# Transposing gathered rows of an expert tile: sixteen block transfers and VectorE in place of four TensorE transposes

## The chip, the core and the metric

The kernel runs on one core of a Trainium2 chip. A core has a matrix engine (TensorE; PE in the profile, PEld its weight loads), a vector engine (VectorE, DVE), a scalar engine (ScalarE, ACT), GpSimd (POOL) and a sync engine (SP) that only waits and issues transfers. Each engine runs its own instructions in order; they meet through semaphores. Sixteen DMA engines move data between the chip's memory and SBUF, the core's on-chip memory of 128 partitions. The metric is the device time of one execution in microseconds (us), lower is better.

## The reference

One layer over 2048 tokens of width 512, in float32: a state-space (Mamba-2) block with a gated MLP, then a mixture of eight experts of which each token uses two. The part that matters here is the second.

```python
def _L0_ffn_ref(x, Wr, Wg, Wu, Wd):          # x: 1 x 2048 x 512, 8 experts, inner width 352
    router_logits = jnp.einsum('bsh,he->bse', x, Wr)
    probs = jax.nn.softmax(router_logits.astype(jnp.float32), axis=-1)
    topk_w, topk_idx = jax.lax.top_k(probs, K)
    topk_w = topk_w / jnp.sum(topk_w, axis=-1, keepdims=True)
    ...
    g = jnp.einsum('bsh,ehi->besi', x, Wg)
    u = jnp.einsum('bsh,ehi->besi', x, Wu)
    h = jax.nn.silu(g) * u
    y = jnp.einsum('besi,eih->besh', h, Wd)
    out = jnp.einsum('bse,besh->bsh', combine.astype(x.dtype), y)
    ...
x = x + _L0_attn_ref(_layernorm(x, axis=-1), ...)      # state-space block and gated MLP
x = x + _L0_ffn_ref(_layernorm(x, axis=-1), L0_ffn_Wr, L0_ffn_Wg, L0_ffn_Wu, L0_ffn_Wd)
```

## The kernel before, in words

The kernel works in three overlapping stages. `mamba` goes over eight blocks of 256 tokens. `feed_forward` goes over four blocks of 512 tokens, each in sixteen chunks of the inner width 2048; its weights pass through three buffers of the tag `mg` (tiles `mg` and `ms`, loaded by SP) and four of `md`. Each `feed_forward` ends with `route`, which normalises the rows (`xn`, line 598), writes them to `xnd` in memory (and to `xnd1` for the first three blocks), computes the router logits with `wr_sb`, and appends each token to the lists of its two experts by indirect scatters on POOL (line 669).

The expert stage computes only what is routed. The lists are cut into tiles of 128 rows of one expert. `table` turns the counts into a table of tiles: `first` has ten tiles (`NS1`) from the first three blocks of tokens, so that they can start while the last block is still routed; `rest` covers what is left, after a load of the lists on SP (line 973). 36 tiles (`NSA`) always run; three more stand under a condition at the end.

A tile s takes these steps:

- `gather` (line 1024, POOL): an indirect transfer fetches 128 rows of 512 values into `xg`, two buffers (tag `row3`).
- `front`: TensorE transposes the four 128 x 128 blocks of `xg` (`transposed`, line 201) into one PSUM bank `pt`, and ScalarE copies them to `xgT` (line 203). `xgT` has the 128 positions of the width on partitions, as the matmuls need.
- `hidden` (lines 1043, 1047, 1048): matmuls `epg` and `epu`, four of each, with the expert's weights `ew` chosen by a register; then Silu on ScalarE and a product on VectorE give `eh`.
- `turned` (lines 1055 to 1058): three transposes of `eh` on TensorE, copied to `ehT` by VectorE and ScalarE.
- `back` (lines 1064, 1069, 1070): three matmuls `epd`, VectorE scales by the token's weight to `ey`, and POOL scatters the rows with an addition into `out`.

`tiles` overlaps them: in iteration s it gathers ahead, does `front` for tile s + 1, the first half of `hidden` for s, `turned` for s - 1, the second half of `hidden`, and `back` for s - 1. `fetch` gathers one tile further than `front`. The last block's routing (`second`) is advanced along with it.

```python
            steps = hidden(s, xT.pop(s))
            next(steps)
            if last:
                hT = turned(s - 1, last[0])
            ...
            now = finish(steps)
            yield
            if last:
                if s < NSA - 1:
                    back(s - 1, hT, last[1])
```

TensorE's instructions stand in the order in which the program is written from block 2 on (`tc.manual_schedule`). The queues of the other engines, SP and POOL included, are ordered by a planner that works with assumed costs, so an instruction that waits holds up what the planner put behind it. The planner also sets the semaphores: transfers issued by SP and ACT take eight completion semaphores in turn, and one that takes a semaphore first waits for the transfer that had it.

Of the kernel before, what the change touches and what calls it, by code (L numbers as in the profile page):

```python
# [9 lines left out]
F32 = mybir.dt.float32  # L10
I32 = mybir.dt.int32
AF = mybir.ActivationFunctionType
ALU = mybir.AluOpType
# [3 lines left out]
P = 128  # L17
T = 2048
D = 512
NK = D // P  # L20
# [12 lines left out]
FC = 128  # L33
NFC = DFF // FC
NE = 8
EI = 352
ET = [(0, 128), (128, 128), (256, 96)]


NS = (2 * T + NE * (P - 1)) // P  # L40

NS1 = 10


NSA = (2 * T + NE * (P // 2)) // P
EW = NK * 2 * EI + len(ET) * D
EPS = 1e-5
# [7 lines left out]
def mamba_mlp_moe(ctx, tc, x, w_in, w_out, w_gu, w_down, par, wr, wg, wu, wd, out):  # L55
# [3 lines left out]
    nc = tc.nc  # L59

    def bc(ap, axis, n):
        ap = ap.unsqueeze(axis)
        shape = list(ap.shape)
        shape[axis] = n
        return ap.to_broadcast(shape)
# [7 lines left out]
    pmlp = ctx.enter_context(tc.tile_pool(name="pmlp", bufs=2, side="right"))  # L73
# [13 lines left out]
    w_o = pw.tile([P, 8, D], F32, name="w_o")  # L87
    wr_sb = const.tile([P, NK, NE], F32, name="wr_sb")

# [6 lines left out]
    def load_w_in(pair):  # L96
# [15 lines left out]
        out=tri, in_=ones, pattern=[[1, P]], compare_op=ALU.is_ge, fill=0.0, base=0, channel_multiplier=-1  # L112
# [3 lines left out]
        out=late, in_=ones, pattern=[[-1, P]], compare_op=ALU.is_gt, fill=0.0, base=0, channel_multiplier=1  # L116
# [3 lines left out]
    nc.gpsimd.memset(eps, EPS)  # L120
    rank = const.tile([P, NE], F32, name="rank")
    nc.gpsimd.iota(rank, pattern=[[-1, NE]], base=NE, channel_multiplier=0, allow_small_or_imprecise_dtypes=True)
    halo = pw.tile([P, 12, 3], F32, name="halo")
    nc.vector.memset(halo, 0.0)
    count = const.tile([P, P], F32, name="count")
    nc.gpsimd.iota(count, pattern=[[1, P]], base=0, channel_multiplier=0, allow_small_or_imprecise_dtypes=True)
    count_hi = const.tile([P, P // NE], F32, name="count_hi")
    nc.vector.tensor_scalar_mul(count_hi, count[:, 0 : P // NE], float(P))
# [4 lines left out]
        out=upto, in_=ones[:, : NE * NE].rearrange("p (e f) -> p e f", e=NE), pattern=[[1, NE], [-1, NE]],  # L133
# [8 lines left out]
    def rsqrt_eps(dst, src, scale=1.0):  # L142

        nc.scalar.activation(dst, src, AF.Sqrt, bias=eps, scale=scale)
        nc.vector.reciprocal(dst, dst)

    def stats(pool, src, dst):
        st = pool.tile([P, 6], F32, name="bn", tag="bn")
        nc.vector.bn_stats(out=st, in_=src)
        nc.vector.bn_aggr(out=dst, in_=st)  # L150
# [26 lines left out]
    def bank(kind, shape, name):  # L177
        pool, tag = use[kind]
        return pool.tile([P, *shape], F32, name=name, tag=tag)
# [17 lines left out]
    def transposed(src, dst, weight=None, kind="tr"):  # L197

        pt = bank(kind, [NK, P], "pt")
        for k in range(NK):  # L200
            nc.tensor.transpose(pt[:, k, :], src[:, k * P : (k + 1) * P], ident)  # L201
        if weight is None:
            nc.scalar.copy(dst, pt)  # L203
        else:
            nc.vector.tensor_tensor(dst, pt, bc(weight, 2, P), ALU.mult)
# [314 lines left out]
    KH = NK // 2  # L520
# [62 lines left out]
    def small(name, *shape):  # L583
        return small_p.tile([P, *shape], F32, name=name, tag=name)

    def route(fb, rows):

        mv2, rs2 = small("mv2", NJ, 2), small("rs2", NJ)
        for j in range(NJ):
            stats(small_p, rows[j], mv2[:, j, :])  # L590
        rsqrt_eps(rs2, mv2[:, :, 1])
        lg, l2, tmp = (small(n, NJ, NE) for n in ("lg", "l2", "tmp"))

        def normed(j):
            t = fb * NJ + j
            nc.scalar.dma_start(out=out[t * P : (t + 1) * P, :], in_=rows[j])
            xn = mid([D], f"xn{t}")
            nc.vector.tensor_scalar(xn, rows[j], mv2[:, j, 0:1], rs2[:, j : j + 1], ALU.subtract, ALU.mult)
            nc.scalar.dma_start(out=xnd[t * P : (t + 1) * P, :], in_=xn)
            if fb < NFB - 1:  # L600
                nc.scalar.dma_start(out=xnd1[t * P : (t + 1) * P, :], in_=xn)
            return xn

        def logits(j, xT):
            pl = bank("d", [NE], f"pl{fb}_{j}")
            for k in range(NK):
                nc.tensor.matmul(pl, xT[:, k, :], wr_sb[:, k, :], start=(k == 0), stop=(k == NK - 1))
            nc.vector.tensor_copy(lg[:, j, :], pl)

        xn = normed(0)  # L610
        yield
        for j in range(NJ):
            if j:
                logits(j - 1, xT)
            xT = mid([NK, P], f"xT{fb}_{j}")
            transposed(xn, xT)
            if j < NJ - 1:
                xn = normed(j + 1)
            yield
        logits(NJ - 1, xT)  # L620

        chosen = [small(n, NJ, NE) for n in ("o1", "o2")]
        m1, m2, *mr = (small(n, NJ) for n in ("rm1", "rm2", "mr1", "mr2"))

        def top(src, mx, mr, oh):

            nc.vector.tensor_reduce(mx, src, AX.X, ALU.max)
            nc.vector.tensor_tensor(tmp, src, bc(mx, 2, NE), ALU.is_equal)
            nc.vector.tensor_tensor(tmp, tmp, bc(rank, 1, NJ), ALU.mult)
            nc.vector.tensor_reduce(mr, tmp, AX.X, ALU.max)  # L630
            nc.vector.tensor_tensor(oh, tmp, bc(mr, 2, NE), ALU.is_equal)

        top(lg, m1, mr[0], chosen[0])
        nc.vector.scalar_tensor_tensor(l2, chosen[0], -3.0e38, lg, ALU.mult, ALU.add)
        top(l2, m2, mr[1], chosen[1])

        wt = [small(n, NJ) for n in ("wt1", "wt2")]
        nc.vector.tensor_tensor(m2, m2, m1, ALU.subtract)
        nc.scalar.activation(m2, m2, AF.Exp)
        nc.vector.tensor_scalar_add(wt[0], m2, 1.0)  # L640
        nc.vector.reciprocal(wt[0], wt[0])
        nc.vector.tensor_tensor(wt[1], m2, wt[0], ALU.mult)


        both, prior = small("both", NJ, NE), small("prior", NJ, NE)
        nc.vector.tensor_tensor(both, *chosen, ALU.add)
        nc.vector.tensor_copy(prior[:, 0, :], before)
        for j in range(1, NJ):
            nc.vector.tensor_tensor(prior[:, j, :], prior[:, j - 1, :], both[:, j - 1, :], ALU.add)
        nc.vector.tensor_tensor(before, prior[:, NJ - 1, :], both[:, NJ - 1, :], ALU.add)  # L650
        yield
        yield
        pr = bank("tr", [NJ, NE], f"pr{fb}")
        nc.tensor.matmul(pr, tri, both, start=True, stop=False)
        nc.tensor.matmul(pr, ones, prior, start=False, stop=True)
        nc.vector.tensor_copy(prior, pr)

        for n in range(2):

            at, to = small("at", NJ), small_p.tile([P, NJ], I32, name=f"to{n}", tag=f"to{n}")  # L660
            nc.vector.tensor_tensor(tmp, chosen[n], prior, ALU.mult)
            nc.vector.tensor_reduce(at, tmp, AX.X, ALU.add)
            nc.vector.scalar_tensor_tensor(at, mr[n], -float(T), at, ALU.mult, ALU.add)
            nc.vector.tensor_scalar_add(at, at, NE * T - 1.0)
            nc.vector.tensor_copy(to, at)
            entry = entries[:, n, fb * NJ : (fb + 1) * NJ, :]
            nc.vector.tensor_copy(entry[:, :, 1], wt[n])
            for j in range(NJ):
                nc.gpsimd.indirect_dma_start(
                    out=writers.pop(), out_offset=bass.IndirectOffsetOnAxis(ap=to[:, j : j + 1], axis=0),  # L670
                    in_=entry[:, j, :], in_offset=None,
                )
            yield
# [240 lines left out]
    ew = pexp.tile([P, NE, EW], F32, name="ew")  # L914
    NG = NK * 2 * EI

    def load_expert(e, part):

        gu = ew[:, e, :NG].rearrange("p (k a n) -> p k a n", k=NK, a=2)
        d = ew[:, e, NG:].rearrange("p (m n) -> p m n", m=len(ET))  # L920
        for lo in (part * EI,) if part < 2 else (NG, NG + 2 * D):
            nc.gpsimd.tensor_copy(ew[: EI - 2 * P, e, lo : lo + 1], newest[: EI - 2 * P, 0:1])
        if part < 2:
            nc.sync.dma_start(out=gu[:, :, part, :], in_=(wg, wu)[part][e].rearrange("(k p) n -> p k n", p=P))
        else:
            nc.sync.dma_start(out=d[:, 0:2, :], in_=wd[e, 0 : 2 * P, :].rearrange("(k p) n -> p k n", p=P))
            nc.sync.dma_start(out=d[: EI - 2 * P, 2, :], in_=wd[e, 2 * P : EI, :])

# [98 lines left out]
        return xg  # L1027

    def front(s, xg):
        xT = wk.tile([P, NK, P], F32, name=f"xgT{s}", tag="a", bufs=4)  # L1030
        transposed(xg, xT)
        return xT

    def hidden(s, xT):
        n, (exp_i, _, _, _), _ = of(s)
        e = nc.tensor.value_load(exp_i[0:1, n : n + 1], min_val=0, max_val=NE - 1)
        w = ew[:, bass.DynSlice(e, 1), :].rearrange("p a n -> p (a n)")
        pg = bank("g", [EI], f"epg{s}")
        pu = bank("u", [EI], f"epu{s}")
# [37 lines left out]
    got, xT = {}, {}  # L1077
# [114 lines left out]
```

## Time and profile before

| what | value |
|---|---|
| time, median of 3 runs | 1545.49 us (1543.01 to 1547.49) |
| the profiled execution | 1548.72 us, span of its instructions 1546.9 us |
| mean granted TensorE clock | 0.991 of full speed |
| busy share of the span | PE 97%, DVE 48%, ACT 48%, POOL 27% |
| expert stage | from about 1231 us to the end |

The profile is of one execution. It lists each instruction's engine, line, operation and its tiles as `out<-in`; `SPq` is SP issuing a transfer, and a transfer's landing is told apart from its issue. A busy TensorE is a row of overlapping matmuls, so the length of one instruction is longer than what it adds. Waits are put down to whoever ended them last.

### The profile page before, as it was taken

The page shows a single profiled execution, that of the slowest core. Times are in us where ns is not written, and L with a number is a line of the kernel's source. Part 1 is how long each engine was busy: PE and PEld are TensorE (multiplying, and loading weights), DVE is VectorE, ACT ScalarE, POOL GpSimd, SP SyncE. Part 2 cuts the span into 40 slices and gives each one's busy share as a digit, 9 for nine tenths or more (in the row PEclk, how much of TensorE's full clock was granted, in tenths as well). Part 3 has the DMA queues.
Part 4 walks back from the last instruction along what each step waited for, and adds up shares of the span by engine and source line. Part 5 has one row for each costly group of instructions (what it writes and reads, how often), then busy time and mean ns, then how long its engine had stood idle before and what let it go on. Part 6 is the DMA issues. An engine that isn't in the chain of part 4 may idle for free. (4 is left out here: it accounts for less than half of the span.)

```text
span 1546.9 us, 18821 instructions
## 1 busy us (share of the span) xinstructions
PE 1501.2 (97%) x6153; PEld 1022.8 (66%) x6153; DVE 747.7 (48%) x1937; ACT 744.1 (48%) x1332; POOL 423.9 (27%) x537
## 2 busy tenths in 40 slices
PE   7999999999999999999999999999999999999996
PEld 6656667677767676766776777666776665566553
DVE  7676866554645564547454553434343432222221
ACT  5888967635764597548646653222221221111110
POOL 3532324424332212141212121311121133333321
PEclk9999999999999999999999999999999999999998
DMA  9444445545554554354335632436878434333332
GB/s 295 146 135 124 136 147 188 188 156 158 169 164 145 173 179 140 104 128 157 123 126 161 186 100 89 93 106 218 292 184 269 150 75 58 69 68 63 63 66 35
DMA packets 128241, 217.54 MB, mean 141 GB/s; under 512 B 12560, under 2 KB 72848, under 8 KB 128144
## 3 DMA queue, kind: packets, MB, share of 16 engines
q1 hardware_dynamic: 105376, 166.34, 35.6%
q0 software_dynamic: 9088, 18.91, 7.2%
q10 hardware_dynamic: 13680, 31.07, 5.4%
q8 instruction: 52, 0.85, 0.2%
q14 instruction: 45, 0.37, 0.1%
HBM read 175.48 MB, written 40.80 MB: 140 GB/s over the span
## 5 line engine op out<-in xcount | busy, mean ns | idle before, releaser
L691 PE MATMUL pd<-md,a 128*128 128x512 f32 x512 | 238.9, 593 | 0.8 <-DVE r L692 0.7
L340 PE MATMUL pm<-hT,wi 128*128 128x256 f32 x768 | 185.7, 387 | 5.2 <-DMA wi<-in_w_in 5.2
L340 PEld LDWEIGHTS pm<-hT,wi 128*128 128x128 f32 x768 | 142.0, 192 | 30.8 <-issue 8.0
L692 DVE TENSOR_TENSOR r<-r,pd 128x512 f32<-128x512 f32 x128 | 87.5, 684 | 151.9 <-PE pd L691 148.4
L691 PEld LDWEIGHTS pd<-md,a 128*128 128x128 f32 x512 | 97.1, 190 | 76.8 <-issue 65.8
L361 DVE SCALAR_TENSOR_TENSOR ca<-pre,params,ca 128x256 f32<-128x256 f32 x288 | 142.4, 553 | 0.3
L707 PE MATMUL py<-h2T,ms 128*128 128x256 f32 x512 | 132.5, 381 | 3.4 <-DMA ms<-late 2.7
L772 POOL TENSOR_TENSOR a<-a,up 128x256 f32<-128x256 f32 x64 | 46.9, 734 | 267.6 <-DVE up L766 234.7
L340 PE MATMUL pz<-hT,wi 128*128 128x256 f32 x512 | 117.0, 381 | 0.0
L490 PE MATMUL po<-w_o,zs 128*128 128x512 f32 x256 | 112.7, 593 | 0.0
L1043 PE MATMUL epg<-ew,xgT 128*128 x288 | 109.0, 460 | 0.2 <-ACT xgT L203 0.2
L707 PEld LDWEIGHTS py<-h2T,ms 128*128 128x128 f32 x512 | 96.1, 191 | 19.2 <-issue 3.1
L1043 PE MATMUL epu<-ew,xgT 128*128 x288 | 108.7, 459 | 0.0
L420 ACT ACT_TABLE_LOAD x75 | 96.2, 1283 | 21.7 <-DVE ncum L285 14.1
L340 PEld LDWEIGHTS pz<-hT,wi 128*128 128x128 f32 x512 | 94.8, 190 | 13.8 <-ACT cum L420 0.8
L1064 PE MATMUL epd<-ew,ehT 128*128 (+1 forms) x216 | 100.6, 602 | 1.0 <-DVE ehT L1057 1.0
L420 ACT ACTIVATE cum<-cum,ncum 128x128 f32<-128x128 f32 x256 | 85.7, 392 | 7.3 <-POOL cum L314 6.0
L490 PEld LDWEIGHTS po<-w_o,zs 128*128 128x128 f32 x256 | 48.4, 190 | 56.1 <-issue 55.0
L752 ACT COPY a<-px 128x256 f32<-128x256 f32 x64 | 23.6, 369 | 126.4 <-PE px L707 113.1
L1024 POOL DMA_INDIRECT xg<-xnd,idx x36 | 35.9, 996 | 163.4 <-PE pt L201 161.2
L203 ACT COPY xgT<-pt 128x512 f32<-128x512 f32 x36 | 21.0, 587 | 116.5 <-PE pt L201 116.5
L422 DVE SCALAR_TENSOR_TENSOR cum<-cum,dt,psc 128x128 f32<-128x128 f32 x256 | 73.1, 341 | 5.0 <-PE psc L414 2.7
(239 smaller groups left out, 2530.4 us busy)
## 6 DMA issues: line engine op xcount, KB each, us to landing
wi<-in_w_in SPq DMA_DIRECT2D x80, 512.0 KB, 3.8
ms<-late SPq DMA_DIRECT2D x48, 512.0 KB, 3.7
mg<-early SPq DMA_DIRECT2D x48, 384.0 KB, 3.7
md<-in_w_down SPq DMA_DIRECT2D x64, 256.0 KB, 4.1
cum<-rowsd SPq DMA_DIRECT2D x32, 512.0 KB, 4.0
late<-ms ACTq DMA_DIRECT2D x16, 512.0 KB, 2.6
ec<-rowsd SPq DMA_DIRECT2D x60, 128.0 KB, 3.4
xnd<-xn ACTq DMA_DIRECT2D x28, 256.0 KB, 3.8
```

The source lines that it names most:

```text
L340: nc.tensor.matmul(pm[:, m, :], w[:, k, m * P : (m + 1) * P], hT[:, k, :], start=(k == 0), stop=(k == NK - 1))
L361: nc.vector.scalar_tensor_tensor(ca, pre[:, m, k : k + TB], cw[:, k : k + 1], ca, ALU.mult, ALU.add)
L420: nc.scalar.activation(lt[:, half, i], lt[:, half, i], AF.Exp, bias=ncum[:, j, h : h + 1])
L422: nc.vector.scalar_tensor_tensor(lt[:, half, i], lt[:, half, i], dt[:, j, h : h + 1], psc[:, half, i], ALU.mult, ALU.mult)
L490: nc.tensor.matmul(po, y[:, m, :], w_o[:, m, :], start=(m == 0), stop=(m == 7))
L691: nc.tensor.matmul(pd, a[:, j * P : (j + 1) * P], d, start=(m == 0), stop=(m == 1))
L692: nc.vector.tensor_tensor(rows[j], rows[j], pd, ALU.add)
L707: nc.tensor.matmul(ps, w[:, k], m[:, k], start=(first and k == 0), stop=(k == KH - 1), skip_group_check=True)
L772: nc.gpsimd.tensor_tensor(a[:, 1], a[:, 1], up, ALU.mult)
L1024: nc.gpsimd.indirect_dma_start(out=xg, out_offset=None, in_=src, in_offset=bass.IndirectOffsetOnAxis(ap=idx[:, n : n + 1], axis=0))
L1043: nc.tensor.matmul(ps, xT[:, k, :], w[:, lo : lo + EI], start=(k == 0), stop=(k == NK - 1))
L1064: nc.tensor.matmul(pd, hT[:n, m, :], w[:n, NG + m * D : NG + (m + 1) * D], start=(m == 0), stop=(m == len(ET) - 1))
```

## The change

`front` no longer uses TensorE. SP issues sixteen transfers from `xg` to a new tile `xq`, each a block of 32 rows by 128 values: rows 32 r to 32 r + 31 of the tile and quarter q of the width go to partitions 32 q to 32 q + 31, place r. Then one VectorE instruction transposes every 32 x 32 block of `xq` into `xgT`. `xq` takes one of the three buffers of the tag `mg`, which the MLP weights had. So that each quarter of a row holds the values that belong on its 32 partitions, the normalised rows are written to `xnd` in the order (q k c) in place of (k q c), and the rows of the router's weights are put into the same order on the host.

```diff
+QD = 32
...
             xn = mid([D], f"xn{t}")
-            nc.vector.tensor_scalar(xn, rows[j], mv2[:, j, 0:1], rs2[:, j : j + 1], ALU.subtract, ALU.mult)
+
+            nc.vector.tensor_scalar(
+                xn.rearrange("p (q k c) -> p k q c", q=P // QD, k=NK),
+                rows[j].rearrange("p (k q c) -> p k q c", q=P // QD, k=NK),
+                mv2[:, j, 0:1], rs2[:, j : j + 1], ALU.subtract, ALU.mult,
+            )
...
     def front(s, xg):
+
+        xq = pmlp.tile([P, NK, KH, FC], F32, name="xq", tag="mg", bufs=3)[:, :KH].rearrange("p a b f -> p (a b) f")
+        blocks = [slice(n * QD, (n + 1) * QD) for n in range(P // QD)]
+        for q, to in enumerate(blocks):
+            for r, of_ in enumerate(blocks):
+                nc.sync.dma_start(out=xq[to, r], in_=xg[of_, q * P : (q + 1) * P])
         xT = wk.tile([P, NK, P], F32, name=f"xgT{s}", tag="a", bufs=4)
-        transposed(xg, xT)
+        nc.vector.transpose(
+            xT.rearrange("p k (r i) -> p r k i", i=QD), xq.rearrange("p r (k c) -> p r k c", k=NK)
+        )
         return xT
...
-        "wr": a["Wr"],
+        "wr": a["Wr"].reshape(NK, P // QD, QD, NE).swapaxes(0, 1).reshape(D, NE),
```

## The prediction

> **What bounds the kernel now.** I read the table of engine time by stretch first, because the change touches one stage, the expert tiles, and the averages of the whole span say little of it. Columns: stretch, its length, busy time with instruction counts of PE, PEld, DVE, ACT and POOL, granted clock, DMA share, GB/s.
>
> ```profile
> 1200.00:1250.00 50.00, 49.76 (x200) 33.30 (x199) 20.02 (x41) 12.86 (x26) 7.05 (x10) 1.00 0.38 126
> 1250.00:1300.00 50.00, 47.31 (x185) 29.31 (x184) 17.83 (x71) 9.82 (x19) 21.44 (x20) 0.97 0.41 70
> 1400.00:1450.00 50.00, 50.00 (x179) 29.82 (x178) 10.18 (x18) 7.87 (x18) 15.55 (x12) 1.00 0.37 64
> ```
>
> From about 1300 us on TensorE has no idle time at all, at full granted clock, while VectorE, ScalarE and the DMA engines are mostly free. A tile costs what TensorE takes for it. So the second view is the timeline of one tile, and of the last ones, where nothing is left to fetch (start, length, engine, line, operation).
>
> ```profile
> 1402.23 0.76 PE L1043 MATMUL epg<-ew,xgT 128*128 x2
> ...
> 1407.29 2.74 PE L1064 MATMUL epd<-ew,ehT 128*128 x6
> ...
> 1409.87 0.60 PE L201 MATMUL pt<-ident,xg 128*128 128x128 f32 x4
> ...
> 1410.31 0.76 PE L1043 MATMUL epg<-ew,xgT 128*128 x2
> ...
> 1520.44 2.74 PE L1064 MATMUL epd<-ew,ehT 128*128 x6
> ...
> 1523.02 0.76 PE L1043 MATMUL epg<-ew,xgT 128*128 x2
> ```
>
> The first gate matmuls of two tiles start 1410.31 - 1402.23 = 8.08 us apart. From the first down matmul to the next gate matmul it is 1410.31 - 1407.29 = 3.02 us with four transposes between, and 1523.02 - 1520.44 = 2.58 us without. The four transposes hold TensorE for 0.44 us a tile, not for their listed 0.60, since matmuls overlap. That is all the change can take from TensorE.
>
> The third view is SP, which gets the new work: its timeline where four issues stand close together, its last issue, and the issue durations by line (min/median/max in ns). The POOL row is the gather of tile 8, the last row the landing times of all gathers.
>
> ```profile
> 1204.75 0.38 SPq L924 DMA_DIRECT2D ew<-in_wu  x1
> 1205.23 0.46 SPq L926 DMA_DIRECT2D ew<-in_wd  x1
> 1205.73 0.46 SPq L927 DMA_DIRECT2D ew<-in_wd  x1
> 1206.28 0.41 SPq L552 DMA_DIRECT2D md<-in_w_down  x1
> ...
> 1288.50 0.33 SPq L973 DMA_DIRECT2D rows<-lists  x1
> ```
> ```profile
> L278 SPq DMA_DIRECT2D rowsd<-rows x8: 318/330/1588, 22.5 to 821.9; - x8
> L279 SPq DMA_DIRECT2D rowsd<-rows_e x8: 373/452/462, 26.9 to 824.0; - x8
> L324 SPq DMA_DIRECT2D ec<-rowsd x60: 445/588/1595, 31.2 to 874.8; - x60
> L530 SPq DMA_DIRECT2D mg<-in_w_gu x16: 327/422/461, 19.4 to 461.4; - x16
> ```
> ```profile
> 1281.57 0.99 POOL L1024 DMA_INDIRECT xg<-xnd,idx  x1 [0.30 <-issue]
> ```
> ```profile
> DMA to landing us min/median/max: 3.3/3.4/7.8
> ```
>
> SP is empty in the expert stage but for one load. An issue takes 0.32 to 0.33 us when SP has rested and 0.42 to 0.46 us right behind another, whether it moves 16 KB (L279) or 128 KB (L530); the gaps between are 0.04 to 0.10 us.
>
> **The change part by part.**
>
> *Removed from TensorE and ScalarE.* 36 tiles by 0.44 us is 15.8 us, all on the path. The ScalarE copy (L203, 0.59 us) goes too and is worth nothing: ScalarE is busy 7.87 of 50 us.
>
> *Added on SP.* Sixteen transfers a tile, each of 32 partitions by 512 bytes, SBUF to SBUF, all issued by SP in order. The trace has no transfer of that kind. Nearest is L279, 32 rows of 512 bytes out of SBUF just behind another transfer: 0.452 us. From below, L530 gives 0.422; from above, L324, into 64 partitions, 0.588. A transfer that waits for the one eight before it (they share eight completion semaphores) may need a wait instruction, so I take the gap halfway between 0.04 and 0.10: 0.07. That is 0.522 a transfer and 16 x 0.522 = 8.35 us a tile. Without the transposes TensorE needs 8.08 - 0.44 = 7.64. So SP, idle before, takes over the beat. I take L279 because its size and its source are the same; both ends stay for the range.
>
> The page "DMA: Bandwidth & Descriptors" of the Trainium skill, under "Issuing engines are not separate DMA queues", calls the sequencer's time to start a DMA usually small relative to the DMA itself. L279 speaks against it here: a 0.45 us issue, sixteen times, is as long as a whole tile. By the page SP would cost nothing and the time would be that of the first rival.
>
> *Where SP starts to matter.* Up to tile 7 there is slack: routing of the last tokens shares TensorE, and tile 0's transfers can start at about 1213.4 us, when the weights whose buffer they take were last read; eight tiles by 8.35 end at 1280. Tile 8's rows cannot come sooner than now: its gather sits in POOL's queue behind the list scatters, starts at 1281.57 and lands up to 7.8 us later, 1289.35. From there SP has 28 tiles (8 to 35) to send: 28 x 8.35 = 233.8, to 1523.2. The last transfer lands some 2.6 us later (the median of L278's landings) and VectorE transposes in 0.69, so tile 35 can start at 1526.5. Now it starts at 1523.02: 3.5 us lost, where TensorE alone would have gained 15.
>
> *VectorE's transpose.* One instruction of 512 elements a partition, 36 times. The nearest rows of this width are 0.55 us (L598) and 0.75 (L1069); I take 0.69. VectorE is busy 10 of 50 us, so its length is covered; without that cover it is 36 x 0.69 = 25 us. Its wait is not: VectorE is in order, and behind a transpose that waits for transfers stand the product eh (L1048), the copy ehT (L1057) and the scaling ey (L1069), for which TensorE's pht and epd and POOL's scatter wait. The copy starts 2.9 us into a tile (1405.12 against 1402.23), so a transpose queued ahead of it is needed up to 5.2 us sooner than TensorE itself needs it. That shifts the phase once, 0 to 5.2 us.
>
> The page "VectorE: DVE Perf Modes", under "Rules for kernel authors", would leave a 128x128 transpose on TensorE, and under "The three transpose paths" gives 390 ns for one in bf16. By that figure (an estimate) the removal would be worth 36 x 4 x 0.39 = 56 us; the timeline shows 15.8.
>
> *Gathers and scatters on POOL.* A gather now waits until sixteen transfers have read its buffer. Its loop through two buffers is transfers 8.35, landing 2.6, gather 3.4: 14.4 us for two tiles, under 2 x 8.35, so it does not set the beat. But the scatters share POOL's queue, and each (1.6 us issue, 4.8 to land) waits for the one before: if one is left over at the end it costs 6.4. For this and the phase together, 0 to 11.6, I take 3, nearer to nothing since scatters have spare time in a tile longer than 6.4.
>
> *Also.* The normalised rows are written in another column order (L598, 0.55 us, perhaps 0.75 with the permuted output): 16 times, under TensorE's work; uncovered, the last four cost 0.8. The router weights' rows are reordered on the host, outside the time. SP's load for the second table (L973, now at 1288.50 after waiting for the list scatters) now stands among the transfers; it waits until about the same moment as tile 8's gather, so it adds no more. The DMA engines, at 0.37, get 256 KB a tile beside the gather's and the scatter's 256 KB each; they stay below full.
>
> *Sum.* 3.5 + 3 = 6.5 us. The profiled execution took 1548.72 us, span 1546.9 and 1.8 around it, and lies 3.2 above the median of 1545.49; set on the median it gives **1552**.
>
> **The rivals.** *TensorE keeps the beat (faster).* If the issues go at L530's 0.422 and a gap of 0.05, a tile takes SP 7.55 us, less than 7.64. Then tile 35 starts about 35 x 0.44 = 15.4 us sooner, and with the 3 us above it ends 12 sooner: 1533.5. For it: several lines show this rate back to back. Against: L279, and every wait instruction. The point that decides between gain and loss is (1523.0 - 3.3 - 3 - 1289.35) / 28 = 8.12 us a tile, 0.508 a transfer.
>
> *A draw.* L279's issue with the small gap only, 0.502, gives 8.03 a tile: 28 x 8.03 = 224.8, tile 35 at 1517.5, 5.5 sooner, less 3: 1543.
>
> *Transfers into few partitions cost what L324's do (much slower).* 0.638 with the gap, 10.2 a tile. Then SP is behind already at tile 8 (1213.4 + 81.6 = 1295), and 28 more end at 1580.6, tile 35 at 1583.9: 61 + 3 slower, 1609. For it: L324 writes parts of the partitions, as the new transfers do. Against: L324 also repeats its source over 64 partitions.
>
> **How the numbers follow.** Forecast (SP sets the beat, 0.51 to 0.57 a transfer) 0.41; its own range 1546 to 1576, by 28 x 16 x 0.05 = 22 us more at the upper end. TensorE keeps the beat 0.27, the draw 0.17, much slower 0.15. A difference of 0.3%, 4.6 us, is about what a measurement of this kernel can tell from none. The draw holds most of "same", with a little of the forecast's lower end; it gives some to faster. Faster 0.29, same 0.17, slower 0.54. The range runs from 1531, just below the first rival, to 1600, which leaves out most of the last.
>
> **What would show it.** On SP the new transfers stand almost without gaps from 1290 on, 8.35 us a tile; TensorE shows idle time each tile that ends on the VectorE transpose, and that one waits for transfers. If TensorE still has 50.00 of 50 and tiles are 7.64 apart, the first rival is right. Issue medians of 0.42, 0.45 or 0.59 choose between the cases. Tile 8 starting much later than 1305, or tiles whose period is neither SP's nor TensorE's, would mean that the queue orders on VectorE or POOL matter more than I allow.

## The result, and the profile after

The change makes the kernel slower: 1622.25 us (1619.74 to 1627.19, four runs) against 1545.82 in the same comparison, a ratio of 1.0497 with a 95% interval of 1.0477 to 1.0517. The forecast was 1552 with a range up to 1600. The sign was right, and so was the mechanism that the forecast put first (SP's issues set the beat of the tiles). The size was not: 76 us in place of 6.5. The profiled execution of after took 1622.13 us, with a span of 1620.3.

The table of engine time by stretch, same columns as before the change:

```profile
1200.00:1250.00 50.00, 47.03 (x161) 29.77 (x160) 19.81 (x40) 9.85 (x20) 5.53 (x9) 0.93 0.42 130
1250.00:1300.00 50.00, 38.84 (x142) 23.12 (x141) 18.20 (x70) 6.43 (x13) 18.13 (x16) 0.93 0.44 85
1400.00:1450.00 50.00, 39.05 (x116) 22.02 (x115) 10.95 (x20) 3.63 (x10) 12.96 (x10) 0.93 0.39 75
```

TensorE, full from 1300 us on before, is now idle for 11 of 50 us, and no other engine column is near 50. The granted clock is lower too, 0.93, but that is not where the time goes: the median gate matmul takes 0.459 us in both profiles, and only 17 of the 576 gate and up matmuls of after took more than 0.6 us. What TensorE waits for is in none of these columns, because issuing a transfer is not counted as busy. SP's timeline shows it (start, length from the first to the last issue of a group, count):

```profile
1212.21 85.19 SPq L1041 DMA_DIRECT2D xq<-xg  x128
1297.78 0.34 SPq L979 DMA_DIRECT2D rows<-lists  x1
1298.26 32.33 SPq L1041 DMA_DIRECT2D xq<-xg  x50
```

The source view of that line, with min/median/max in ns, and who waits for it most (us, times):

```profile
L1041 SPq DMA_DIRECT2D xq<-xg x576: 507/589/1683, 1212.2 to 1587.7; - x192
...
  DVE xgT L1043: 254.2, 36
...
DMA to landing us min/median/max: 1.7/2.1/7.4
```

An issue takes 0.589 us and the next one starts 0.04 to 0.05 later: 32.33 / 50 = 0.647 with the occasional long issue in it, 0.634 without. Sixteen of them are 10.14 us. A tile's first gate matmul follows that of the tile before after 10.36 us on average (tiles 12 to 34; before the change 8.08). SP stands in front of everything: it is busy issuing from 1212.21 to 1588.25 and waits, over its 576 transfers, for next to nothing (2.8 us in three waits for earlier transfers).

The end of the run shows the rest (timeline of the last tiles; brackets: idle before, and who ended it):

```profile
1584.49 3.76 SPq L1041 DMA_DIRECT2D xq<-xg  x6
...
1589.54 0.71 DVE L1043 STREAM_TRANSPOSE xgT<-xq 128x512 f32<-128x512 f32 x1 [8.03 <-DMA xq<-xg]
1590.18 0.48 DVE L1062 TENSOR_TENSOR eh<-eh,epu 128x352 f32<-128x352 f32 x1
...
1590.71 0.55 PE L1069 MATMUL pht<-ident,eh 128*128 128x128 f32 x3 [2.35 <-DVE eh L1062]
...
1593.47 2.74 PE L1078 MATMUL epd<-ew,ehT 128*128 x6
...
1596.05 0.76 PE L1057 MATMUL epg<-ew,xgT 128*128 x2
```

The last row is tile 35's first matmul, at 1523.02 before: 73.0 us later, and the span is 73.4 longer, so after this point almost nothing more is lost. Read backwards: SP's last issue ends at 1588.25 (1584.49 + 3.76), its data is there by 1589.54, when the transpose starts, the transpose of tile 35 ends at 1590.25, and only 5.8 us later does its first matmul start. In between, VectorE first forms the product `eh` of tile 33, which stood in its queue behind the transpose; TensorE, in program order, then runs `pht` of 33, the second half of 34 and the down matmuls of 33.

So 1596.05 = 1212.21 (SP's start) + 365.2 (576 x 0.634) + 10.8 (issues of up to 1.68 us that recur about every fifth tile, the load of line 979, a few short waits) + 1.3 (landing) + 0.7 (transpose) + 5.8 (the two tiles still in flight).

### The profile page after: what moved, and what is told of

Read it like the earlier page. It is cut to its first block, busy times and chain, and to the rows that moved or that the text cites. A ratio compares the mean times of both kernels' runs of the same rounds, so it can differ in the third digit from the quotient of the medians.

```text
span 1620.3 us, 19352 instructions
## 1 busy us (share of the span) xinstructions
PE 1504.8 (93%) x6009; PEld 1011.9 (62%) x6009; DVE 766.2 (47%) x1973; ACT 722.0 (45%) x1296; POOL 427.6 (26%) x537
## 5 line engine op out<-in xcount | busy, mean ns | idle before, releaser
L1043 DVE STREAM_TRANSPOSE xgT<-xq 128x512 f32<-128x512 f32 x36 | 25.6, 711 | 254.2 <-DMA xq<-xg 254.2
L1072 ACT COPY ehT<-pht 96x128 f32<-96x128 f32 x36 | 9.4, 262 | 295.6 <-DVE ehT L1071 295.6
L1078 PE MATMUL epd<-ew,ehT 128*128 (+1 forms) x216 | 107.0, 634 | 26.6 <-DVE ehT L1071 26.6
L713 PEld LDWEIGHTS py<-h2T,ms 128*128 128x128 f32 x512 | 96.1, 191 | 19.8 <-issue 3.8
L1078 PEld LDWEIGHTS epd<-ew,ehT 128*128 128x128 f32 (+1 forms) x216 | 42.3, 202 | 76.1 <-issue 38.3
```

The costliest lines, as they stand in the source:

```text
L713: nc.tensor.matmul(ps, w[:, k], m[:, k], start=(first and k == 0), stop=(k == KH - 1), skip_group_check=True)
L1043: nc.vector.transpose(xT.rearrange("p k (r i) -> p r k i", i=QD), xq.rearrange("p r (k c) -> p r k c", k=NK))
L1078: nc.tensor.matmul(pd, hT[:n, m, :], w[:n, NG + m * D : NG + (m + 1) * D], start=(m == 0), stop=(m == len(ET) - 1))
```

## The experiments

The theories: **A**, the price lies in the issue and comes from writing only part of the partitions; **B**, it lies in the transport of the data; **C**, it lies in the issue and comes from having SBUF at both ends; **D**, the order of VectorE's queue, not SP, sets the beat. A ratio is to the kernel before on the same chip.

### price: fourteen shapes of transfer by themselves

The kernel before, with eight SP transfers to an unused tile in tiles 6 to 33, each kind in turn (the planner issues some of them much earlier, from 58 us on); some of the kinds (`ident` is 128 x 128 in SBUF, `x` the input in memory, `q0`, `q1` the first and second 32 partitions):

```diff
+            lambda r: nc.sync.dma_start(out=w[:, r], in_=ident),
+            lambda r: nc.sync.dma_start(out=w[:96, r], in_=ident[:96]),
...
+            lambda r: nc.sync.dma_start(out=w[q0, r], in_=ident[q1]),
+            lambda r: nc.sync.dma_start(out=w[q0, r], in_=x[r * 32 : (r + 1) * 32, 0:P]),
+            lambda r: nc.sync.dma_start(out=w[q1, r], in_=x[r * 32 : (r + 1) * 32, 0:P]),
+            lambda r: nc.sync.dma_start(out=w[:, r], in_=x[r * P : (r + 1) * P, 0:P]),
...
+            lambda r: nc.sync.dma_start(out=probed[r], in_=ident),
+            lambda r: nc.sync.dma_start(out=w[0:16, r], in_=ident[0:16]),
```

> The kernel before, with eight further SP transfers in each of the tiles 6 to 33 whose results nobody uses; fourteen shapes, each on a line of its own, 512 bytes a row. Theory A (the price lies in the issue, and belongs to transfers that write part of SBUF's partitions): back to back, the transfers into 32 or 64 partitions take 0.59 us on SP, whether they come from SBUF or from memory; those of 128 or 96 partitions, and those from 32 partitions into memory, 0.42 to 0.46. Theory B (SP is held up by transport: many small packets beside gathers and scatters): here, with half the transfers and none of 10 us without a pause, all of them take 0.45 or less. Theory C (SBUF on both sides is the price): 0.59 for all that go from SBUF to SBUF, the 128-partition ones included, and 0.45 for all with memory on one side. Under all three the time stays within 5 us of the kernel before, since TensorE waits for none of it.

Measured, SP's timeline (start, length of a row of eight issues):

```profile
1208.01 5.01 SPq L1091 DMA_DIRECT2D probe<-ident  x8
1214.30 3.58 SPq L1092 DMA_DIRECT2D probe<-in_x  x8
...
1221.71 3.91 SPq L1094 DMA_DIRECT2D probe<-in_x  x8
1225.66 4.96 SPq L1098 DMA_DIRECT2D probe<-ident  x8
...
1236.11 5.08 SPq L1086 DMA_DIRECT2D probe<-ident  x8
```

From SBUF to SBUF eight issues take 4.96 to 5.08 us where no long issue falls among them, into 32 partitions (L1091), 16 (L1098) or 96 (L1086); from memory to SBUF 3.58 and 3.91, into 32 (L1092) and 128 (L1094). The source views give the medians:

```profile
L1085 SPq DMA_DIRECT2D probe<-ident x16: 465/600/878, 1230.7 to 1296.7; - x16
L1089 SPq DMA_DIRECT2D probe<-ident x16: 544/590/1328, 1251.9 to 1317.2; - x16
L1092 SPq DMA_DIRECT2D probe<-in_x x16: 333/421/1822, 1214.3 to 1273.0; - x16
L1097 SPq DMA_DIRECT2D probed<-ident x16: 422/432/808, 58.4 to 94.0; - x16
```

128 partitions (L1085) cost what 32 cost (L1089); memory at one end, as source or as target (L1097), takes 0.16 us off the issue. That is C; A's partitions play no part. It holds for these shapes, 512 bytes a partition. Memory at one end does not by itself make an issue cheap: in before, L324 (0.588) and one more row, of 256 KB a transfer, read from memory and cost what SBUF to SBUF costs here.

```profile
L541 SPq DMA_DIRECT2D ms<-in_w_gu x16: 550/581/677, 19.8 to 469.4; - x16
```

What those two rows have in common with SBUF at both ends, no run shows. The single execution took 1553.37 us, 7.6 more than the median of before, where at most 5 had been expected. The time was lost between tiles 6 and 7 (23.4 us, 13.2 before), where the load of the lists stood behind added transfers (issued at 1293.86, before at 1288.50).

### wide4 and memory16: fewer transfers, and another source

`wide4` moves the same bytes in four transfers; the rows stay on their partitions, so the blocks are not where they belong and the result is not the layer's:

```diff
-        for q, to in enumerate(blocks):
-            for r, of_ in enumerate(blocks):
-                nc.sync.dma_start(out=xq[to, r], in_=xg[of_, q * P : (q + 1) * P])
+        for r in range(NK):
+            nc.sync.dma_start(out=xq[:, r], in_=xg[:, r * P : (r + 1) * P])
```

> The changed kernel with four transfers of 128 partitions by 512 bytes in place of the sixteen: the same bytes, the same buffers, the same VectorE transpose and the same waits, but rows stay on their partitions, so the blocks are not where they belong. Theory A (issue): four issues are 2 to 2.5 us a tile, TensorE sets the beat again at 7.64 us a tile, and the time is 1530 to 1538, below the kernel before. Theory B (transport of the bytes): the time stays near 1600. Theory D (the order of VectorE's queue, where the transpose stands two tiles ahead in front of the product, sets the beat): tiles stay well over 8.08 us apart and the time is 1560 or more.

Measured: 1525.25 us (1524.44 to 1528.09), ratio 0.9872 (0.9845 to 0.9898). The source view, and the stretch in the steady part:

```profile
L1040 SPq DMA_DIRECT2D xq<-xg x144: 464/600/1169, 1208.5 to 1467.4; - x144
```
```profile
1400.00:1450.00 50.00, 50.00 (x167) 29.41 (x166) 15.45 (x27) 4.62 (x13) 16.41 (x13) 1.00 0.49 100
```

The time is below the 1530 to 1538 that theory A gave. The issues cost the same 0.600 us each; there are four, 2.5 us a tile. TensorE is full again, the tiles stand 7.64 us apart, and all bytes are moved and transposed as in after. So B and D fall: neither the bytes nor VectorE's queue sets the beat. The run also shows what the removal is worth when SP does not set the beat: 20 us. In the traces, 11.9 us of it come from tile 7 to tile 35 (27 x 0.44) and 5.1 between tiles 0 and 7, most of that between tiles 6 and 7 (9.1 us, 13.2 before). The rest lies before tile 0, where profiled executions of one kernel differ too: that of before is 3.2 us above its median.

`memory16` keeps sixteen transfers of 32 x 128 but reads them from a fixed block of the kernel's input in memory, so the rows are the wrong ones:

```diff
-                nc.sync.dma_start(out=xq[to, r], in_=xg[of_, q * P : (q + 1) * P])
+                nc.sync.dma_start(out=xq[to, r], in_=x[r * QD : (r + 1) * QD, q * P : (q + 1) * P])
```

> The changed kernel with its sixteen transfers of the same shape and number, but their source is a fixed block of the layer's input in memory in place of the gathered rows in SBUF, so the rows are the wrong ones and no transfer waits for a gather. The price list gave 0.420 us an issue and 0.465 from start to start when memory is on one side, 0.589 and 0.634 when SBUF is on both. Theory C (the price belongs to SBUF on both sides): 16 x 0.465 = 7.44 us a tile, under TensorE's 7.64, so TensorE sets the beat and the time is 1525 to 1545. If the number or the size of the transfers were the cause (theories A and B), each issue stays at 0.59 and the time at 1610 or more.

Measured: 1538.36 us (1536.6 to 1541.68), ratio 0.9964 (0.9946 to 0.9981); tiles 7.89 us apart.

```profile
L1041 SPq DMA_DIRECT2D xq<-in_x x576: 310/419/1617, 1210.1 to 1503.9; - x192
```

Number, size, targets and queue are those of after; the source alone differs, the issue falls from 0.589 to 0.419, and the ratio from 1.0497 to 0.9964: more than the whole loss goes. These transfers need not wait for gathers either, but SP waited for next to nothing in after, so that is not where the time comes from. So the source is the cause. The tiles stand 7.89 us apart and not 7.64: from 1330 us on the starts of SP's transfers lie 0.485 us apart on average, long issues included, and 16 x 0.485 = 7.76 is still a little more than TensorE needs.

### twelve and split: SP's share cut by a quarter and by half

`twelve` joins every second pair of blocks of the upper half of the partitions into one transfer of 64 partitions, twelve a tile (their rows are not where they belong):

```diff
+        half = [slice(0, HD), slice(HD, P)]
+        for r, of_ in enumerate(blocks):
+            for q in range(2):
+                nc.sync.dma_start(out=xq[blocks[q], r], in_=xg[of_, q * P : (q + 1) * P])
+            nc.sync.dma_start(out=xq[half[1], r], in_=xg[half[r // 2], (2 + r % 2) * P : (3 + r % 2) * P])
```

> The changed kernel with twelve transfers a tile: eight of 32 partitions as before, and four of 64 partitions for the upper half of SBUF, of which the rows are not where they belong. All of xq is written. Theory A: 12 x 0.634 = 7.6 us a tile on SP, just what TensorE needs (7.64), so nearly all of the loss goes with a quarter of the transfers: 1535 to 1552. Theory B (transport): the bytes are the same, 1600 or more. Theory D (queue order): less than 15 us gained on the changed kernel.

Measured: 1542.95 us (1539.98 to 1548.48), ratio 0.9983 (0.9966 to 1.0001). SP now needs 12 x 0.634 = 7.61 us a tile, just less than TensorE's 7.64, and from tile 7 on the tiles stand 7.64 us apart. Most of the gain is eaten at one place: between tiles 6 and 7 there are 19.9 us, 13.2 before. (Another 2.4 go at the end, where 26.3 us follow tile 35's first matmul, 23.9 before; POOL still has scatters left over there.) A wait of TensorE in 1275 to 1305 us, and POOL's timeline, first in `twelve` and then in before:

```profile
PE pi L984 <- DMA rows<-lists: 8.5, 1, 8.5
```
```profile
1271.91 0.95 POOL L1030 DMA_INDIRECT xg<-xnd,idx  x1 [6.35 <-DMA xq<-xg]
...
1275.09 1.00 POOL L675 DMA_INDIRECT lists<-entries,to  x1 [0.30 <-DVE step L957]
```
```profile
1271.26 1.00 POOL L669 DMA_INDIRECT lists<-entries,to  x1 [0.30 <-DVE ehT L1057]
```

TensorE's next instruction by program order belongs to the second table, and waits for the load of the lists, issued at 1292.39, 3.9 us later than before (1288.50). The load did not stand behind transfers: SP was idle from 1287.5 to 1291.7 and waited for the list scatters on POOL. These began 3.8 us later than before, since a gather ahead of them in POOL's queue waited until SP's transfers had read its buffer. TensorE, which had been 3.2 us ahead of before at tile 6, now waited 8.5 us for the lists (2.7 before), and the six down matmuls behind the wait took 5.41 us (4.52 before at this place, 2.74 elsewhere).

`split` leaves SP the odd r and gives the even ones to ScalarE's queue:

```diff
-                nc.sync.dma_start(out=xq[to, r], in_=xg[of_, q * P : (q + 1) * P])
+                by = nc.sync if r % 2 else nc.scalar
+                by.dma_start(out=xq[to, r], in_=xg[of_, q * P : (q + 1) * P])
```

> The changed kernel with every second transfer issued by ScalarE's queue in place of SP's: same transfers, same data, eight on each. Theory A (a queue's issue): SP needs 8 x 0.634 = 5.1 us a tile, ScalarE 5.1 and its own 1.2 for Silu and copies, both under 7.64; TensorE sets the beat: 1533 to 1550, the upper part if ScalarE's Silu has to stand behind transfers that wait. Theory B (transport, or one descriptor generator shared by both queues): 1600 or more, and each issue about twice as long when both queues issue.

Measured: 1553.89 us (1553.28 to 1555.9), ratio 1.0059 (1.0037 to 1.0081). The source view:

```profile
L1042 SPq DMA_DIRECT2D xq<-xg x288: 507/589/1869, 1211.1 to 1499.5; - x144
L1042 ACTq DMA_DIRECT2D xq<-xg x288: 514/601/1562, 1211.1 to 1499.5; - x144
```

That is a little above the 1533 to 1550 that theory A gave. The two queues issue side by side without slowing each other, and from tile 10 on the tiles stand 7.64 us apart. But ScalarE is in order too: a transfer that waits for its gather (11.0 us from 1281.06 on) holds the copy of `ehT` and the activation behind it. A wait of ScalarE in 1270 to 1320 us, and TensorE's wait for that copy:

```profile
ACT ehT L1073 <- DMA xq<-xg: 16.1, 1, 16.1
```
```profile
1297.94 2.08 PE L1079 MATMUL epd<-ew,ehT 96*128 x2 [7.47 <-ACT ehT L1073]
```

Between tiles 4 and 10 the tiles stand up to 17.2 us apart. From tile 10 to tile 35 the run gains 10.6 us (24 x 0.44), and 18.9 are lost between tiles 0 and 10.

### late_turn: the transpose later in VectorE's queue

The transpose of tile s + 1 is queued behind the copy `ehT` of tile s - 1, so that it cannot hold `eh` of s - 1:

```diff
+            if s + 1 in turns:
+                with tc.issue_after(copied) if last else ExitStack():
+                    turns.pop(s + 1)()
```

> The changed kernel with the VectorE transpose of tile s + 1 queued behind the copy ehT of tile s - 1, in place of two tiles ahead and in front of a product; the sixteen transfers stay. In the changed kernel 6 us lie between the end of the last transpose (1590.2) and the first matmul of tile 35 (1596.05), since the transpose held up the product of tile 33. If that order costs its share once, as a shift of phase: 4 to 6 us less than the changed kernel, 1616 to 1618. If it costs something in every tile (theory D): 20 us or more less. If the phase is made up elsewhere: no difference. The tiles stay 10.2 to 10.4 us apart under the first and the last.

Measured: 1613.4 us (1612.15 to 1615.34), ratio 1.0452 (1.0432 to 1.0471), 8.9 us less than after (7 by the two ratios), where 4 to 6 had been expected for a shift and 20 or more for a cost in every tile. Tiles are still 10.4 us apart, so the order shifts the phase once and doesn't set the beat. Tile 35's first matmul now starts 2.0 us after the start of its transpose (1586.2 and 1588.2), where it was 6.5: 4.5 us. The transpose itself starts 3.3 us earlier (1589.5 in after): SP began 5.1 us earlier (1207.1 against 1212.2), since the planner placed the first transfers elsewhere, and kept a part of that. The second was not meant. Together they are 7.8, about what was measured.

### quarters: no transfers on SP at all

Four indirect gathers on POOL fetch the quarter rows straight into the blocked layout, with their own list of row numbers (`idxq`, made by TensorE and VectorE with the tables):

```diff
+        for r in range(NK):
+            nc.gpsimd.indirect_dma_start(
+                out=xq[:, r], out_offset=None, in_=parts,
+                in_offset=bass.IndirectOffsetOnAxis(ap=idxq[:, r, n : n + 1], axis=0),
+            )
```

> No block transfers at all: each tile is gathered by four indirect transfers on POOL of 128 quarter rows (512 bytes) that land where the VectorE transpose needs them; the indices for them (four times the row, plus the quarter) come from four more small matmuls in each table. If SP's issue is the whole cause, TensorE sets the beat at 7.64 us a tile: POOL needs 4 x 1.28 for the gathers and 1.9 for the scatter, 7.0 us a tile, so it just keeps up, and the time is 1525 to 1540, below the kernel before. If a quarter gather costs POOL more than 1.45 us from start to start, POOL sets the beat: 1550 or more.

Measured: 1562.23 us (1558.38 to 1563.32), ratio 1.0116 (1.0098 to 1.0134). A quarter gather takes POOL 0.95 us, 1.26 from start to start, and POOL with its 36 of 50 us busy still leaves TensorE the beat of 7.64 from tile 11 on. So neither expectation held: the beat is the first one's, the time the second's. The time goes before that: 22.5 us from tile 1 to 2 (10.6 before), 19.8 from 5 to 6 (8.1 before), 15.4 from 9 to 10 (8.1 before). In the first of these POOL issues quarter gathers in a row without a pause (1224.16 to 1241.48), while TensorE waits for `eh` and VectorE and ScalarE stand at waits that the profile names only "remote". That POOL's row of gathers causes them was not tested.

### mixed, mixed_late: the change only where its queues are free

`mixed` leaves tiles 0 to 9 to TensorE (rows of the first table kept in the old column order) and turns tiles 10 to 35 as in `split`:

```diff
     def front(s, xg):
+        if s < NS1:
+            xT = wk.tile([P, NK, P], F32, name=f"xgT{s}", tag="a", bufs=4)
+            transposed(xg, xT)
+            return xT
```

> Tiles 0 to 9 (first table) are turned by TensorE as in the kernel before, from rows kept in the old column order (one more VectorE instruction for each of 12 token tiles); tiles 10 to 35 go by sixteen transfers shared by SP's and ScalarE's queues and the VectorE transpose, as in split. The output is the reference's. If split lost its time only in tiles 5 to 9, where ScalarE's other work and the second table's load stood behind transfers, then nothing is lost there now, and 26 tiles gain 8.08 - 7.64 = 0.44 us each: 11.4 us less than before, 1534, with tiles 7.64 us apart from tile 10 on. If holding ScalarE behind transfers costs wherever transfers begin, a gap of 8 to 15 us appears around tiles 9 to 12 and the time is 1542 to 1550. If the two queues together are too slow in the steady stretch, the period is above 8.08 and the time above 1546.

Measured: 1542.1 us (1535.67 to 1545.38), ratio 0.9983 (0.997 to 0.9997). From tile 12 on the period is 7.64. The second expectation held for the rest: 33.0 us from tile 9 to tile 12, where 22.9 were due, as the transfers begin. The waits in 1300 to 1345 us:

```profile
ACT ehT L1078 <- DMA xq<-xg: 28.0, 4, 11.2
```

`mixed_late` has three edits on top: tiles 10 to 12 by SP alone, then 5 of 16 transfers on ScalarE and 11 on SP, and the late transpose.

> As mixed (tiles 0 to 9 by TensorE), but tiles 10 to 12 go by SP alone, of the later tiles' sixteen transfers ScalarE issues 5 and SP 11, and the VectorE transpose is queued behind the ehT copy of the tile two before. The output is the reference's. If mixed lost its gain because ScalarE's copies and activations stood behind transfers that waited for gathers (28.0 us of waits of the ehT copy between 1300 and 1345 us), the gap there goes and the time is 1533 to 1537. If the gap has another cause it stays: 1540 to 1544.

Measured: 1546.45 us (1541.47 to 1549.79), ratio 1.0011 (0.9994 to 1.0028). The gap stayed (35.0 us from tile 10 to tile 13, where 22.9 were due), and the time is above both expectations. Fewer transfers on ScalarE don't free it: one that waits is enough. ScalarE's first transfer of tile 13 waits 6.6 us for earlier transfers and then 2.7 us for its gather (from 1313.85 to 1323.31), and TensorE waits 4.0 us for the copy of `ehT` behind it.

### thirds and thirds3: SP alone, with time to spare

`thirds` uses no ScalarE queue. Tiles 0 to 9 and then every third are turned by TensorE, the other 18 by SP's sixteen transfers:

```diff
+def by_pe(s):
+    return s < NS1 or s % 3 == 0 and s < NSA
```

> Tiles 0 to 9 and every third tile after them (12, 15, ... 33) are turned by TensorE, from rows kept in the old column order; the other 18 tiles go by sixteen transfers on SP alone, and the VectorE transpose is queued behind the ehT copy of the tile two before. The output is the reference's. SP then has 2 x 16 x 0.634 = 20.3 us of issues for three tiles, TensorE 2 x 7.64 + 8.08 = 23.4. If SP's rate is the only limit of the changed kernel (theory C), TensorE keeps the beat and the gain is 18 x 0.44 = 7.9 us: 1536 to 1538. If transfers cost something even where SP has time to spare (gathers held by them, the waits on VectorE), the time stays at 1544 or above.

Measured: 1604.93 us (1599.99 to 1605.52), ratio 1.037 (1.0343 to 1.0397). A clear miss: SP has 20.3 us of issues for 23.4 us of TensorE, and yet three tiles take 30.8 on average (tiles 12 to 34). SP's waits in 1366 to 1425 us:

```profile
SPq L1062 <- DMA xg<-xnd,idx: 22.0, 4, 5.8
```

With a TensorE tile between, the two row buffers no longer alternate among tiles with transfers. A gather waits until SP's transfers of the tile just before have read its buffer, and the next transfers wait for that gather: 10.14 of issues and 5.5 of gather, one after the other, 15.6 a tile with transfers, and two such tiles in three. `thirds3` puts the gathers of these tiles into the unused half of the tile that holds `xq`, which has three buffers:

```diff
-        xg = row(f"xg{s}")
+        xg = row(f"xg{s}") if by_pe(s) else broad(s)[:, KH:].rearrange("p a b f -> p (a b f)")
```

> As thirds, with one edit: the gathers of the tiles that go by transfers are written into the free half of the tile that holds xq (three buffers) in place of the two row buffers. In thirds SP waited 5.5 us for a gather at each tile with transfers (22.0 us in four waits between 1366 and 1425 us), because with a TensorE tile between, a gather waits for the transfers of the tile just before, and the next transfers wait for that gather. If that loop is the whole cause of its 60 us, SP's 20.3 us for three tiles are covered, the waits go and the time is 1536 to 1539. If a transfer tile costs 15 us for another reason, the period stays at 10 us a tile and the time at about 1600.

Measured: 1539.43 us (1536.5 to 1544.17), ratio 0.9973 (0.9957 to 0.9989); that is 65 us off `thirds`, all from the one edit, and just above the 1536 to 1539 expected if the loop was the whole cause. Of the versions that compute the whole layer it is the fastest, 4.7 us below the kernel before. TensorE is full:

```profile
1400.00:1450.00 50.00, 50.00 (x169) 29.37 (x168) 13.51 (x24) 6.26 (x16) 15.69 (x13) 1.00 0.51 94
```

`mixed_late3` is the same edit in `mixed_late`:

> As mixed_late, with the same edit of the gathers' buffers. If the gap around tiles 10 to 13 (12 us) was the same loop, with ScalarE's copies behind transfers that waited for gathers, it goes and the time is 1533 to 1537. If ScalarE is held by the issues themselves, it stays at 1542 to 1547.

Measured: 1548.84 us (1536.56 to 1554.67), ratio 1.0028 (1.0008 to 1.0047). The gap from tile 10 to 13 shrank from 35.0 to 27.6 us (22.9 were due), but now the later tiles pay: 8.10 us on average, some 7.64 and some 8.4 to 9.1. (One of the twelve executions took 1536.56, the other eleven 1547.01 or more; why is open.) ScalarE's waits between 1290 and 1540 us:

```profile
ACT ehT L1103 <- DMA xq<-xq: 131.4, 16, 11.8
```

So the loop explains part of the gap only. What remains goes with ScalarE's queue: in 1380 to 1410 us TensorE waits three times, 0.6 to 0.8 us each, for the copy that ScalarE's transfers hold. `thirds3`, with the same buffers but on SP alone and with every third tile left to TensorE, has no such waits.

## Why the prediction was right and wrong

**The step that failed** is the price of a transfer, in the part "Added on SP": "Nearest is L279, 32 rows of 512 bytes out of SBUF just behind another transfer: 0.452 us", with 0.07 of gap 0.522. Measured: 0.589 and 0.045, 0.634. L279 has the number of rows, the bytes and the source of the new transfers, but writes to memory; no row of before has SBUF at both ends, and `price` and `memory16` show that for transfers of this shape this, and not the number of partitions, sets the issue. The reason given for the row, "because its size and its source are the same", named two features that did not settle it: the other end counts. The forecast's reading of before, 0.42 to 0.46 right behind another, also left out L541 with 0.581, a second row as dear as L324. The gap went the other way, 0.045 for 0.07: no wait instruction was needed in most places.

**What the step does to the sum.** At 0.634 SP issues without a pause from tile 0 on, and the slack "up to tile 7" that the forecast gave it does not exist. The forecast's own chain, so corrected, is 1213.4 + 576 x 0.634 + 2.6 + 0.7 + 3 = 1584.9 for tile 35, against 1529.5 as it stood. That is 55 of the 66.5 us between forecast and trace.

**The other 11** are 10.8 of long issues and waits on SP, which the forecast had at nothing, and 2.8 more of phase, less 1.2 of earlier start and 1.3 of quicker landing. The phase was foreseen as "0 to 5.2", as one shift and not one a tile; it was taken, together with the scatters, at 3 and measured 5.8, above its range, and `late_turn` shows both that it is a shift and its size (4.5 back).

**The mechanism** was right: the new transfers stand without gaps on SP, and TensorE idles. The point of decision, 0.508 a transfer, is bracketed by the runs: `memory16` at 0.465 to 0.485 is a little faster than before, after at 0.634 slower.

**The rivals.** "TensorE keeps the beat" has the right condition (`twelve`, `wide4`: 7.64 a tile as soon as SP needs less) and did not apply. "Transfers into few partitions cost what L324's do" had 0.638, nearly the measured 0.634, and 1609. Its price was right by luck, for its reason was wrong: from SBUF, 128 partitions cost the same, and from memory into 32 partitions an issue costs 0.42. Why L324, from memory into 64 partitions, has 0.588 stays open. It had the least chance, 0.15, and the range left out most of it.

**Queues.** "It adds no more", of SP's load for the second table, held for after, where tile 8 was late anyway. What the forecast had wrong there is the time of the list scatters: it left them where they were before, but they share POOL's queue with gathers that now wait for transfers, and began at 1279.74 in place of 1271.26. In after SP came to the load only at 1297.78 and did not have to wait for them; in `twelve`, where SP kept up, the late scatters are more than half of the 6.7 us lost between tiles 6 and 7. The loop through two gather buffers was rightly judged harmless for after (36 tiles in a row), and `thirds` shows how near it was: one tile of another kind between breaks the alternation and costs 60 us. The scatters left over at the end cost 0.4: from tile 35's first matmul to the end of the span it is 24.3 us against 23.9. The column order of `xn` shows nowhere.

**The rule of the page** "DMA: Bandwidth & Descriptors" of the Trainium skill, "Issuing engines are not separate DMA queues", calls the time to start a DMA usually small relative to the DMA. Here a transfer is issued in 0.589 us and lands 2.1 us after its issue starts (medians), so for one transfer it may pass; for sixteen that overlap, the issue is 10.14 us a tile and nearly the whole loss. The rule that a second engine saves only the sequencer's time agrees with `split`: that saving brought the steady beat back to 7.64.

## What to carry to other kernels

Price an added transfer by its issue on the queue that sends it, times their number, and take the price from a row with the same kind of memory at **both** ends; if the profile has no such row, keep the dearest row as a serious case, even where its shape looks unlike. Before moving small transfers to an idle queue, compare the sum of issues per round with the beat of the engine that is to be relieved: here sixteen at 0.634 lost 76 us, where four (which leave the blocks in the wrong places) gained 20. And a queue in order, ScalarE's too, that holds one waiting transfer holds everything behind it, so spreading transfers over a working engine can cost more than it saves. The same goes for POOL: a gather that waits for its buffer delays the scatters queued behind it.

## What the runs showed of the hardware

- An issue with SBUF at both ends, 512 bytes a partition, takes 0.59 to 0.60 us, 0.63 to 0.64 from start to start, for 16, 32, 64, 96 or 128 partitions alike; the same shapes with memory at one end take 0.42 to 0.43 (`price`, `memory16`). Other shapes from memory took 0.58 to 0.59 in before (L324, L541).
- SP and ScalarE issue side by side: 0.589 and 0.601 us in `split`, against 0.589 for SP alone in after.
- An indirect gather of 128 quarter rows takes POOL 0.95 us; one of 128 whole rows 1.00.
- The VectorE transpose of 128 x 512 in float32 takes 0.711 to 0.715 us, all 36 times in after.
